# Opening, routing and first score rows of a recurrent attention and experts layer: statistics in pairs, score rows set between the routing's steps

## The chip, the cores and the metric

The kernel runs on one core of one Trainium2 chip. The metric is the device time of one execution in microseconds (us); the time before is the median of 3 runs. Engines: PE (TensorE, matmuls and turns, that is transposes by a matmul with the identity), DVE (VectorE), ACT (ScalarE), POOL (GpSimd), SP (SyncE, which here only issues transfers). ACT and POOL issue transfers too.

## The reference, cut to what matters

```python
x = L0_attn_x                                   # (8, 1024, 256), f32
xn = layernorm(x)
# attention over the 4 heads of each token (not over tokens)
q, k, v = ((xn @ W + b).reshape(b, s, h, d) for W, b in ((Wq, bq), (Wk, bk), (Wv, bv)))
qr, qi, kr, ki = q * cos(phase), q * sin(phase), k * cos(phase), k * sin(phase)
scores = (einsum('bshd,bsgd->bshg', qr, kr) + einsum('bshd,bsgd->bshg', qi, ki)) / sqrt(d)
out = einsum('bshg,bsgd->bshd', softmax(scores), v)
s = swapaxes(out, 1, 2).reshape(b, s, h * d) @ Wo + bo
# 8 experts, each token goes to its best 2
r = (einsum('btd,ed->bte', xn, router_w) + router_b) / max(temperature, 0.1)
for _ in range(3):                              # Sinkhorn
    r = r - logsumexp(r, axis=-1); r = r - logsumexp(r, axis=-2)
gates = normalised(exp(r)); vals, idx = top_k(gates, 2)
expert(e) = (relu(xn @ wg[e]) * (xn @ wp[e])) @ wo[e]
g = silu(xn + sum of the two chosen experts, weighted by normalised vals)
result = x + s * g
```

## The kernel before, in words

The 8192 tokens are 64 tiles of 128 rows; four tiles are a block, so there are 16 blocks. All arithmetic is f32, and the trace shows each f32 matmul as two records (a turn as one). The core's work comes in five stages.

**Set-up** (`fetch_setup`, `setup_scores`): small tensors and w_qk (the weights of queries and keys) are loaded. From the phases a 4 by 4 mix of heads for each column is made (`mixrow`), and from mix, biases and turned weights a linear map `lin` (256 rows by 8 + 16 columns): one product of a normalised row with `lin` gives the 8 routing scores and the parts of the 16 head scores that are linear in the row. In L263 to L285 those 16 columns are made by matmuls of four columns each, with a turned 128x128 piece of the weights as the stationary side.

**Opening** (`prepare`, `linear`; 16 blocks): for a block, bn_stats and bn_aggr (DVE L391, L392) give mean and variance of the rows, ACT takes the square root (L393), DVE the reciprocal and the shift (L396, L397); the rows are normalised in place by DVE (L408) and ACT (L403) in turns, PE turns them (L412), ACT copies the turned tile out of PSUM (L415), and POOL issues the stores of the turned rows (xT_d, from block 3 on) and of the normalised rows (xn_d). Each four blocks `linear` runs `lin` over them (L434), turns the result back (L445) and adds the offsets into `lg` (L448). x_0 to x_6 lie in the pool "prep", x_7 to x_11 in buffers of the attention, x_12 to x_15 in a pool "tail" that takes the space of the set-up. Behind the opening the list of entries in memory is filled with padding (L1097), and xn_d is copied to z_d (L1102).

**Routing** (`route`, `order`): 14 steps on one [128, 64, 8] tensor, nearly all on DVE, with three ACT functions (Exp L489, Ln L492, Exp L499, each with a table load) and four sums or maxima over all rows on POOL (L496, L507). `order` works out, for each token and choice, its place in the experts' list; `place` pieces (L643) and POOL's 128 indirect stores (`scatter`, L646) write the list, 8 stores to a piece. Beside it `setup_values` folds Wv and Wo into w_vo: turns of w_v (L295), matmuls pw (L329), ACT copies (L338), and the bias b_vo. Its tiles w_v, wT_v, w_o, bo_all lie in buffers of the attention (tags qk, u, junk).

**Attention** (`score`, `soften`, `value`; a generator `att_gen` whose yields are its steps). A tile's scores are nine steps: four of matmuls py (L666) with an ACT copy into qk (L673), one of four products (DVE L679), four of mixed keys kx (DVE L704) with their products (L679). There are two qk buffers, two kx buffers, and two PSUM buffers for py and pw together (tag "y"). A block behind, a tile's values are three steps: matmuls pu (L749), DVE adds (L756), matmuls po_s (L781), ACT copy. `run(att_gen, n)` sets n steps at that place of the program: 32 behind the first `place` piece, 15 behind each of the other 15, and 13: 270 steps ahead of the experts. The other steps are spread among the experts.

**Experts** (`experts`): 71 groups of 256 list entries; rows are gathered by POOL, three matmuls with their weights, and an indirect add into z_d. At the end `finish` joins x, attention and experts block by block.

**What sets the order.** The program is reordered when it is built: on each engine an instruction is put where it is expected to be ready, and among the ready ones the earlier in the program goes first. So the memset of L317, written in `setup_values`, runs at 7.49 us, and one pair of the matmuls of the first values (L749) at 97.03 us, between pw. `with tc.issue_after(ins)` keeps the instructions in its block behind `ins` on their engine. On the chip each engine then works in that order.

Of the kernel before, what the change touches and what calls it, by code (L numbers as in the profile page):

```python
# [9 lines left out]
F32 = mybir.dt.float32  # L10
AF = mybir.ActivationFunctionType
ALU = mybir.AluOpType
# [18 lines left out]
def recurrent_kernel(  # L31
# [127 lines left out]
    LATE = 3  # L159
    KEPT = 3  # L160
# [15 lines left out]
    def setup_scores(pool, rows, rw):  # L176
# [45 lines left out]
        mbk = pool.tile([P, KD, H, H], F32, name="mbk")  # L222
        mbq = pool.tile([P, KD, H, H], F32, name="mbq")
# [23 lines left out]
        for c in range(KD):  # L247
            nc.vector.tensor_scalar(mix[:, c], mix[:, c], 1.0 / math.sqrt(D), None, ALU.mult)
            nc.vector.tensor_tensor(mbk[:, c], mix[:, c], second(bkT, c), ALU.mult)
            nc.vector.tensor_tensor(mbq[:, c], mix[:, c], first(bqT, c), ALU.mult)  # L250
            nc.vector.tensor_tensor(mbb[:, c], mbk[:, c], first(bqT, c), ALU.mult)
# [9 lines left out]
        nc.vector.tensor_copy(off[:, E:], pl[:, :HH])  # L261
        lk = pool.tile([P, KD, H, H], F32, name="lk")
        for which, m in ((0, mbk), (1, mbq)):  # L263
            pl = ps_tr.tile([P, 512], F32, tag="tr", name=f"pl_lin_{which}")
            for k in range(KD):
                for a in range(H):
                    at = (k * H + a) * H
                    for c in range(KD):
                        nc.tensor.matmul(
                            pl[:, at : at + H],  # L270
                            wT[which][:, a, c, k * P : (k + 1) * P],
                            m[:, c, a] if which == 0 else m[:, c, :, a],
                            start=(c == 0),
                            stop=(c == KD - 1),
                        )
            flat = pl[:, : KD * HH]
            if which == 0:
                nc.vector.tensor_copy(lk.rearrange("p k h g -> p (k h g)"), flat)
            else:
                nc.vector.tensor_tensor(  # L280
                    lin[:, :, E:NL].rearrange("p k (h g) -> p k h g", h=H),
                    lk,
                    flat.rearrange("p (k g h) -> p k h g", k=KD, g=H),
                    ALU.add,
                )  # L285
        return bvT

    def turned(wT, part, name):

        for h in range(H):  # L290
            pt = ps_tr.tile([P, 512], F32, tag="tr", name=f"ptr_{name}_{h}")
            for c in range(KD):
                for k in range(KD):
                    at = c * D + k * P
                    nc.tensor.transpose(  # L295
                        pt[:, at : at + P], part(k, h)[:, c * P : (c + 1) * P], ident
                    )
            copy = nc.scalar.copy if h % 2 else nc.vector.tensor_copy
            copy(wT[:, h].rearrange("p c e -> p (c e)"), pt)

    def setup_values(bvT):

        w_v = att.tile([P, KD, HD], F32, tag="qk", name="w_v")
        with tc.issue_after(newest["rstd"].ins):
            nc.scalar.dma_start(w_v, wv.rearrange("(k p) n -> p k n", p=P))
        wvT = att.tile([P, H, KD, D], F32, tag="qk", name="wT_v")
        w_o = []
        for n in range(2):
            t = att.tile([P, R, D], F32, tag="u", name=f"w_o_{n}")
            half = wo[n * R * P : (n + 1) * R * P]  # L310
            with tc.issue_after(newest["rstd"].ins):
                nc.scalar.dma_start(t, half.rearrange("(k p) n -> p k n", p=P))
            w_o += [t[:, k] for k in range(R)]
        bo_all = att.tile([P, D], F32, tag="junk", name="bo_all")
        nc.gpsimd.dma_start(bo_all[:1], bo.unsqueeze(0))
        share = att.tile([P, D], F32, tag="junk", name="bo_share")
# [3 lines left out]
        turned(wvT, lambda k, h: w_v[:, k, h * D : (h + 1) * D], "wT_v")  # L320
        yield
        for i in range(R):
            for k in range(KD):
                for half in range(2):
                    pw = ps_y.tile([P, 512], F32, tag="y", name=f"pw_{i}_{k}_{half}")
                    for gg in range(2):
                        g = half * 2 + gg
                        for c in range(KD):
                            nc.tensor.matmul(  # L329
                                pw[:, gg * D : (gg + 1) * D],  # L330
                                wvT[:, g, c, k * P : (k + 1) * P],
                                w_o[i * KD + c],
                                start=(c == 0),
                                stop=(c == KD - 1),
                            )

                    with tc.issue_after(newest["shares"].ins) if i >= R // 2 else nullcontext():
                        nc.scalar.copy(w_vo[:, k, i, half * 512 : (half + 1) * 512], pw)  # L338
                yield
# [32 lines left out]

    def prepare(blk: int, pool):
# [10 lines left out]
        stats = small.tile([P, TB, 6], F32, tag="stats", name=f"stats_{blk}")  # L384
        mv = small.tile([P, TB, 2], F32, tag="mv", name=f"mv_{blk}")
        rstd = small.tile([P, TB], F32, tag="rstd", name=f"rstd_{blk}")
        shift = small.tile([P, TB], F32, tag="shift", name=f"shift_{blk}")
        for t in range(TB):

            with tc.issue_after(newest["trig"].ins) if not blk else nullcontext():  # L390
                nc.vector.bn_stats(stats[:, t, :], xt[:, t, :])  # L391
            nc.vector.bn_aggr(mv[:, t, :], stats[:, t, :])  # L392
        norm = nc.scalar.activation(rstd, mv[:, :, 1], AF.Sqrt, bias=eps)  # L393
        if blk < 8:
            newest["rstd"] = norm
        nc.vector.reciprocal(rstd, rstd)  # L396
        nc.vector.scalar_tensor_tensor(shift, mv[:, :, 0], -1.0, rstd, ALU.mult, ALU.mult)  # L397
# [30 lines left out]
    def linear(blk: int, pool):  # L428
# [15 lines left out]
        for t in range(TB):  # L444
            nc.tensor.transpose(  # L445
# [10 lines left out]
    def route(pool, hot, entries):  # L456
# [32 lines left out]
        nc.scalar.activation(ex, la, AF.Exp)  # L489
# [54 lines left out]
    def order(pool, hot, keep, placed):  # L544
# [4 lines left out]
        before = pool.tile(full, F32, name="o_before")  # L549
# [488 lines left out]
    turned_rows, x_tiles, all_scored = {}, {}, []  # L1038
# [36 lines left out]
    with tc.tile_pool(name="prep", bufs=2) as prep:  # L1075
        with tc.tile_pool(name="setup", bufs=1) as setup:
# [7 lines left out]
            bvT = setup_scores(setup, *small_rows)  # L1084
            prepare(0, prep)
        with tc.tile_pool(name="tail", bufs=1) as tail:
            for blk in range(12, T // TB):
                fetch_rows(blk, tail, f"x{blk}", 1)
            for blk in range(1, 4):
                prepare(blk, prep)  # L1090
            linear(0, prep)
            for blk in range(4, T // TB):
                prepare(blk, prep)
                if blk % 4 == 3:
                    linear(blk - 3, prep)
# [6 lines left out]
    copied = nc.sync.dma_start(z_d[: B * S], xn_d[: B * S])  # L1102
    tc.add_to_no_dep_group("padding", copied.ins)
    nc.sync.dma_start(
        z_d[B * S :].rearrange("(p m) d -> p m d", m=M),
        blank.unsqueeze(1).to_broadcast([P, M, D]),
    )
    with tc.tile_pool(name="routing", bufs=1) as routing:
        hot = routing.tile([P, E, K, T], F32, name="hot")
        entries = routing.tile([P, K * T * 2 + LE], F32, name="entries")  # L1110
        nc.vector.memset(entries, 0.0)
        for n in range(K):
            nc.vector.tensor_copy(pairs_of(entries)[:, n, :, 0], ids)

        keep = routing.tile([P, E, K * T], F32, name="keep")
        nc.vector.memset(keep, 1.0)
        nc.vector.memset(keep[:, :, :1], 0.0)

        values = setup_values(bvT)
        for n, _ in enumerate(route(routing, hot, entries)):  # L1120
            if n > 2:
                run(values, 1)

        with tc.issue_after(newest["columns"].ins):
            for m in range(M):
                pad = nc.gpsimd.indirect_dma_start(
                    xn_d,
                    bass.IndirectOffsetOnAxis(ap=padding[:, m : m + 1], axis=0),
                    blank,
                    None,  # L1130
                )
                tc.declare_no_dep(pad.ins, group="padding", reason="rows behind those copied")
                tc.add_to_no_dep_group("padding", pad.ins)
        placed = []
        run(order(routing, hot, keep, placed))
        run(values)
        put = scatter(entries, placed[0])
        next(put)
        run(att_gen, 32)
        for _ in put:  # L1140
            run(att_gen, 15)
        run(att_gen, 13)
# [67 lines left out]
```

## Time and profile before

| what | value |
|---|---|
| median of 3 runs | 1700.5 us (1699.61 to 1701.88) |
| the profiled execution | 1709.65 us, span 1707.8 us |
| PE busy | 1638.0 us, 96% |
| DVE busy | 1204.1 us, 71% |
| ACT, POOL busy | 429.7 us, 638.3 us |
| mean granted clock of PE | 0.978 |
| first turn of a block (PE L412) | 33.02 us |
| last addition into lg (DVE L448) | 87.37 us |
| first step of the routing (DVE L482) | 91.80 us |
| first place piece (DVE L643) | 148.09 us |
| first fetch of the experts' entries (POOL L859) | 396.33 us |
| 500 to 1500 us | PE busy 997.5 of 1000 us |

Times in the trace count from the first instruction; the device time of the same execution is 1.85 us more than its span. The granted clock is the share of full speed that the throttle gave PE. A "wait" is the idle time of an engine ahead of an instruction, with what ended it; it says nothing of cost where that engine isn't the one that sets the end.

### The profile page before, as it was taken

How to read it: one execution, taken by the hardware profiler on the slowest of the kernel's cores; microseconds unless marked ns; L12 is line 12 of the kernel's file. 1: busy time of each engine (PE TensorE's matmuls, PEld its weight loads, DVE VectorE, ACT ScalarE, POOL GpSimd, SP SyncE). 2: the span in 40 equal slices, each digit the busy share in tenths (PEclk: the TensorE clock that was granted, in tenths of full speed). 3: DMA queues.
4: the chain of work that ended last, by engine and by line, in shares of the span. 5: the costliest groups of instructions: out<-in, count | busy, mean ns of one | idle time of the engine just before them, and what ended most of it. 6: DMA issues, size and time to landing. Idle time of an engine off the chain costs nothing.

```text
span 1707.8 us, 22900 instructions
## 1 busy us (share of the span) xinstructions
PE 1638.0 (96%) x7697; PEld 1008.0 (59%) x7697; DVE 1204.1 (71%) x3704; ACT 429.7 (25%) x814; POOL 638.3 (37%) x599
## 2 busy tenths in 40 slices
PE   6897899999999999999999999999999999999986
PEld 5373344444666666766666666666666666767632
DVE  5769999997667566665757657576675756655776
ACT  3741212121222212222222222222222222222131
POOL 0312466566333434333434234343333433442212
PEclk8798999999999999999999999999999999999998
DMA  8993022114544544544544545455455445455489
GB/s 268 360 352 114 28 61 64 60 50 124 152 117 125 141 127 115 163 123 112 156 110 109 151 137 135 124 121 145 121 133 148 121 116 143 121 136 139 138 272 317
DMA packets 149161, 245.38 MB, mean 144 GB/s; under 512 B 15465, under 2 KB 93585, under 8 KB 148913
## 3 DMA queue, kind: packets, MB, share of 16 engines
q1 hardware_dynamic: 105648, 162.32, 29.6%
q0 software_dynamic: 41376, 77.38, 19.9%
q10 hardware_dynamic: 2016, 4.20, 0.7%
q8 instruction: 62, 1.02, 0.2%
q14 instruction: 59, 0.48, 0.1%
HBM read 176.85 MB, written 75.37 MB: 148 GB/s over the span
## 4 chain that ended last, share of the span: by engine, by line
PE 79%; DVE 14%; DMA 3%; issue 1%; ACT 1%; another core or an unknown queue 1%; POOL 0%; SPq 0%; ACTq 0%; POOLq 0%
PE py L666 23%; PE po L925 13%; PE pg L909 12%; PE pp L909 12%; PE pu L749 10%; DVE junk L679 5%; DVE kx L704 3%; PE po_s L781 2%; DVE w L768 2%; PE ptr_g L897 2%; DMA fz<-z_d 1%; PE po_s L776 1%; PE ptr_x L412 1%; DMA fo<-in_L_attn_x_dram 1%; DVE u L756 1%
## 5 line engine op out<-in xcount | busy, mean ns | idle before, releaser
L666 PE MATMUL py<-w_qk,xTa 128*128 128x512 f32 x1024 | 480.2, 605 | 15.9 <-ACT qk L673 14.3
L938 POOL DMA_INDIRECT z_d<-y,row x136 | 233.4, 1716 | 663.5 <-ACT y L935 642.8
L679 DVE CUSTOM_DVE_ANT_0 junk<-qk,kx,lg 128x256 f32<-128x256 f32 x768 | 323.9, 481 | 0.1
L666 PEld LDWEIGHTS py<-w_qk,xTa 128*128 128x128 f32 x1024 | 191.7, 193 | 213.8 <-issue 185.2
L679 DVE CUSTOM_DVE_ANT_0 junk<-qk,lg 128x256 f32<-128x256 f32 x256 | 113.6, 481 | 268.9 <-ACT qk L673 263.5
L673 ACT COPY qk<-py 128x512 f32<-128x512 f32 x256 | 149.2, 585 | 492.6 <-PE py L666 429.6
L909 PE MATMUL pg<-xgT,wg 128*128 128x256 f32 x1088 | 264.3, 385 | 0.2
L909 PE MATMUL pp<-xgT,wp 128*128 128x256 f32 x1088 | 260.6, 381 | 0.3 <-DVE hid L918 0.3
L749 PE MATMUL pu<-w_vo,xTa 128*32 128x512 f32 x2048 | 258.3, 598 | 1.1 <-DVE u L756 1.1
L925 PE MATMUL po<-wd,hid 128*128 128x256 f32 x1088 | 257.7, 382 | 0.0
L909 PEld LDWEIGHTS pg<-xgT,wg 128*128 128x128 f32 x1088 | 201.9, 190 | 84.1 <-issue 41.5
L925 PEld LDWEIGHTS po<-wd,hid 128*128 128x128 f32 x1088 | 203.2, 190 | 68.1 <-issue 44.4
L704 DVE TENSOR_TENSOR kx<-qk,mixrow 128x1024 f32<-128x1024 f32 (+1 forms) x256 | 233.8, 952 | 0.1
L909 PEld LDWEIGHTS pp<-xgT,wp 128*128 128x128 f32 x1088 | 204.4, 190 | 39.0 <-ACT hid L917 7.5
L646 POOL DMA_INDIRECT list_d<-entries,place x128 | 144.3, 1128 | 129.3 <-DVE place L643 94.7
L918 DVE TENSOR_TENSOR hid<-pp,hid 128x512 f32<-128x512 f32 x136 | 93.4, 687 | 138.1 <-PE pp L909 127.2
L768 DVE SCALAR_TENSOR_TENSOR w<-u,sc,w 128x256 f32<-128x256 f32 x444 | 185.9, 477 | 1.0
L872 POOL DMA_INDIRECT xg<-xn_d,row x136 | 151.6, 1115 | 57.1 <-issue 47.1
L917 ACT ACTIVATE hid<-pg 128x512 f32<-128x512 f32 x136 | 81.2, 597 | 297.2 <-PE pg L909 272.9
L749 PEld LDWEIGHTS pu<-w_vo,xTa 128*32 128x32 f32 x2048 | 58.8, 109 | 135.9 <-issue 128.2
L935 ACT ACTIVATE y<-po,entry 128x256 f32<-128x256 f32 x136 | 57.1, 470 | 256.2 <-PE po L925 251.6
L756 DVE TENSOR_TENSOR u<-pu,b_vo 128x512 f32<-128x512 f32 x128 | 86.2, 685 | 27.7 <-PE pu L749 27.4
(212 smaller groups left out, 999.7 us busy)
## 6 DMA issues: line engine op xcount, KB each, us to landing
wg<-in_L_ffn_wg_dram SPq DMA_DIRECT2D x68, 512.0 KB
wp<-in_L_ffn_wp_dram SPq DMA_DIRECT2D x68, 512.0 KB
wd<-in_L_ffn_wo_dram SPq DMA_DIRECT2D x68, 512.0 KB
list_d<-empty POOLq DMA_DIRECT2D x1, 9088.0 KB
x<-in_L_attn_x_dram SPq DMA_DIRECT2D x16, 512.0 KB
xn_d<-x POOLq DMA_DIRECT2D x16, 512.0 KB
s_d<-s_out SPq DMA_DIRECT2D x56, 128.0 KB
fo<-in_L_attn_x_dram SPq DMA_DIRECT2D x14, 512.0 KB
```

Of the source, the lines that this page charges most:

```text
L646: put = nc.gpsimd.indirect_dma_start(list_d, bass.IndirectOffsetOnAxis(ap=piece[:, c : c + 1], axis=0), entries[:, at * 2 : at * 2 + LE], ...
L666: newest["score"] = nc.tensor.matmul(py, xT[:, t, k], w[:, k, cols], start=(k == 0), stop=(k == KD - 1),)
L673: nc.scalar.copy(flat[:, cols], py)
L679: newest["dot"] = nc.vector.tensor_tensor_reduce(junk, qk[:, 0, h], k, 1.0 / math.sqrt(D), lg[:, tile_no, E + at : E + at + 1], ALU.mult, ...
L704: nc.vector.tensor_tensor(kx[:, :w], k, mixrow[:, at : at + w].unsqueeze(2).to_broadcast([P, w, 2, D]), ALU.mult,)
L749: nc.tensor.matmul(pu[i * J : (i + 1) * J, :], xT[:, t, k, i * J : (i + 1) * J], w_vo[:, k, i, cols], start=(k == 0), stop=(k == KD - 1),)
L756: nc.vector.tensor_tensor(u[:, cols], pu, b_vo.rearrange("p g d -> p (g d)")[:, cols], ALU.add)
L768: nc.vector.scalar_tensor_tensor(w[:, h], part, share, w[:, h], ALU.mult, ALU.add)
L872: nc.gpsimd.indirect_dma_start(xg[:, m], None, xn_d, bass.IndirectOffsetOnAxis(ap=row[:, m : m + 1], axis=0),)
L909: nc.tensor.matmul(dst[:, f], w[:, k, at : at + P], xgT[:, k], start=(k == 0), stop=(k == KD - 1),)
L925: nc.tensor.matmul(po[:, m], hid[:, f, m * P : (m + 1) * P], wd[:, f], start=(f == 0), stop=(f == KF - 1),)
L938: add = nc.gpsimd.indirect_dma_start(z_d, bass.IndirectOffsetOnAxis(ap=row[:, m : m + 1], axis=0), y[:, m], None, compute_op=ALU.add,)
```

## The change

**Set-up.** The matmuls of the linear map are turned round: the 4-column pieces, set in zeroed strips of 32 columns (`strips`), are the stationary side, and the turned weights move, 256 columns wide; the four heads go to four strips of 32 PSUM rows. ACT copies the result, PE turns it (four turns), DVE takes the columns out.

```diff
+        strips = att.tile([P, 2, KD, H, LW], F32, tag="mixer", name="strips")
+        nc.vector.memset(strips, 0.0)
...
+        for which in range(2):
+            for c in range(KD):
+                for a in range(H):
+                    nc.tensor.matmul(
+                        pl[a * LW : (a + 1) * LW, which],
+                        strips[which][:, c, a],
+                        wT[which][:, a, c],
+                        start=(c == 0),
+                        stop=(c == KD - 1),
+                    )
+        lT = rest.tile([P, 2, D], F32, tag="lT", name="lin_T", bufs=1)
+        nc.scalar.copy(lT, pl)
...
-        for which, m in ((0, mbk), (1, mbq)):
-            pl = ps_tr.tile([P, 512], F32, tag="tr", name=f"pl_lin_{which}")
-            for k in range(KD):
-                for a in range(H):
-                    at = (k * H + a) * H
-                    for c in range(KD):
-                        nc.tensor.matmul(
-                            pl[:, at : at + H],
-                            wT[which][:, a, c, k * P : (k + 1) * P],
...
```

**Opening.** The statistics leave `prepare` and become `measure`, which is called four blocks ahead; square root, reciprocal and shift are done for two blocks at once.

```diff
+    def measure(blk: int, pool):
+
+        pair, GT = blk // PAIR, PAIR * TB
...
+        if blk % PAIR == PAIR - 1:
+            norm = nc.scalar.activation(rstd, mv[:, :, 1], AF.Sqrt, bias=eps)
+            if blk < 2 * GROUP:
+                newest["rstd"] = norm
+            nc.vector.reciprocal(rstd, rstd)
+            nc.vector.scalar_tensor_tensor(shift, mv[:, :, 0], -1.0, rstd, ALU.mult, ALU.mult)
...
-            for blk in range(1, 4):
+            for blk in range(T // TB):
                 prepare(blk, prep)
-            linear(0, prep)
-            for blk in range(4, T // TB):
-                prepare(blk, prep)
-                if blk % 4 == 3:
-                    linear(blk - 3, prep)
+                if blk + GROUP < T // TB:
+                    measure(blk + GROUP, prep)
+                if blk % GROUP == GROUP - 1:
+                    linear(blk - GROUP + 1, prep)
+                if blk == GROUP:
+                    fetched_values = fetch_values(prep)
```

**Values.** w_v (in two loads) and w_o (two loads) are fetched into the slots of x in "prep" by `fetch_values`, wT_v into two more of them, bo_all into the slot of lT; `hot`, `keep` and `o_before` of the routing lie in slots of xT. The pool "prep" now lasts until the routing is done, and the routing's own pool takes the space of "tail". The matmuls pw are kept behind the last turn of `linear`, and the copies of w_vo behind an Exp of the routing.

```diff
+        w_v = [whole([P, HD], f"w_v_{k}") for k in range(KD)]
+        for k in range(KD):
+            with tc.issue_after(newest["rstd"].ins):
+                nc.scalar.dma_start(w_v[k], wv[k * P : (k + 1) * P])
...
+                            with tc.issue_after(newest["logits"].ins):
+                                nc.tensor.matmul(
...
-                    with tc.issue_after(newest["shares"].ins) if i >= R // 2 else nullcontext():
+                    done = (i * KD + k) * 2 + half
+                    behind = newest["shares" if done > 4 else "first"]
+                    with tc.issue_after(behind.ins) if done > 1 else nullcontext():
                         nc.scalar.copy(w_vo[:, k, i, half * 512 : (half + 1) * 512], pw)
```

Here "logits" is the last turn in `linear`, "first" the routing's first Exp, "shares" its second.

**Score rows.** Two steps of the attention are set behind each of the routing's 14 steps, and 28 fewer behind the first `place` piece; the 270 steps ahead of the experts stay 270.

```diff
             for n, _ in enumerate(route(routing, hot, entries)):
+
+                run(att_gen, 2)
                 if n > 2:
                     run(values, 1)
...
             put = scatter(entries, placed[0])
             next(put)
-            run(att_gen, 32)
+            run(att_gen, 32 - 2 * (n + 1))
             for _ in put:
                 run(att_gen, 15)
             run(att_gen, 13)
```

## The prediction, made before the changed kernel had run

> **What bounds the kernel now.** I read the chain of waits first, then busy time by stage, then the waits of the first 135 us engine by engine. The chain's shares by engine:
>
> ```profile
> PE 79%; DVE 14%; DMA 3%; issue 1%; ACT 1%; another core or an unknown queue 1%; POOL 0%; SPq 0%; ACTq 0%; POOLq 0%
> ```
>
> TensorE ends most of the span, and VectorE's 14% lies mostly ahead of the experts. Four stages show where (columns: stage, its length, busy us and instructions of each engine, granted clock, DMA share, GB/s):
>
> ```profile
> 33.00:88.00 55.00, 43.87 (x222) 23.41 (x223) 39.64 (x184) 38.73 (x82) 17.24 (x29) 0.75 0.91 342
> 88.00:132.00 44.00, 41.19 (x245) 28.38 (x243) 29.59 (x50) 17.61 (x28) 5.48 (x7) 1.00 1.00 353
> 132.00:205.00 73.00, 60.26 (x167) 24.89 (x168) 71.47 (x261) 14.43 (x27) 26.41 (x22) 0.88 0.17 58
> 205.00:396.00 191.00, 185.14 (x836) 79.43 (x834) 187.12 (x631) 40.27 (x78) 117.94 (x107) 1.00 0.20 59
> ```
>
> The opening (33 to 88) fills no compute engine: PE 43.9 of 55 us, DVE 39.6, ACT 38.7, while the DMA engines are at 0.91. In the routing (88 to 132) PE is full with the value weights, and DVE works 29.6 of 44. In 132 to 205 it is the other way round: DVE is full with score rows, PE idles 12.7 us and has only 0.88 of its clock. From 205 on both are full, and behind 396 PE alone (199 of each 200 us). So whatever lets DVE finish its part ahead of 205 earlier arrives at the end undiminished; but only as far as PE keeps up. The waits of DVE and of PE from 20 to 135 us (total, times, longest):
>
> ```profile
> DVE rstd L396 <- ACT rstd L393: 7.4, 8, 3.2
> ...
> DVE r_cm L506 <- ACT r_ex L499: 3.4, 1, 3.4
> DVE r_cs L511 <- POOL r_cs L507: 2.7, 3, 0.9
> DVE r_rs L491 <- ACT r_ex L489: 2.5, 1, 2.5
> DVE r_la L494 <- ACT r_rs L492: 2.4, 1, 2.4
> ...
> DVE entries L1111 <- DMA xn_d<-x: 1.5, 1, 1.5
> DVE r_la L498 <- POOL r_cg L496: 0.8, 1, 0.8
> ```
> ```profile
> PE ptr_x L412 <- ACT rstd L393: 6.6, 4, 1.7
> ```
>
> The routing's steps wait 11.8 us (3.4 + 2.7 + 2.5 + 2.4 + 0.8) for ACT and POOL with nothing else on DVE; in the opening PE waits 6.6 us for a block's standard deviation. The third item is in PE's timeline (start, us, instructions):
>
> ```profile
> 26.20 6.96 PE L269 MATMUL pl_lin<-mbq,wT 128*128 128x4 f32 x32
> 33.02 1.95 PE L412 MATMUL ptr_x<-ident,x 128*128 128x128 f32 x8
> ...
> 47.88 1.09 PE L412 MATMUL ptr_x<-ident,x 128*128 128x128 f32 x8
> ```
>
> The 64 narrow matmuls of L269 hold the first turn of a block back to 33.0 us, though its rows were normalised by 26.9.
>
> **Part 1: the linear map by strips.** Removed: 64 recorded matmuls, 22.4 to 33.2 us. Added: 32 records (each f32 matmul shows as two), 32 columns by 256, in four column strips. The nearest row is L749, same strips, twice as wide: 0.112 us a record, so 0.056, or 1.8 us (3.6 at half clock). Then a 0.59 us ACT copy, 8 records of turning (1.0 to 2.0 us) and two DVE steps of 0.2. The turns of block 0 need not wait for the last four, so they start at 22.4 + 1.8 to 3.6, say 25.5: 7.5 us earlier. The memset of the strips is some 0.5 us of DVE (384 columns took 0.38), in its wait for the first x.
>
> **Part 2: statistics four blocks ahead, in pairs.** The bn_stats and bn_aggr stay 128. Square root, reciprocal and shift fall from 16 of each to 8 of each: ACT saves 8 x 0.3 = 2.4 us, DVE 8 x (0.18 + 0.15) = 2.6 at most, as they overlap. PE's 6.6 us for rstd go. Engines alone would thus end the opening 14 us earlier. The transfers don't allow all of it: by the last store 16 x 0.52 (x) + 2.1 (w_qk) + 2.1 (w_v, w_o) + 16 x 0.52 (xn_d) + 13 x 0.52 (xT_d) = 27.8 MB must have moved; 9.0 of them had by 30 us (230, 355 and 312 GB/s). The remaining 18.8 MB take 45 us at the best slice of 10 us (414 GB/s) and 49 at 380: the last store lands at 75 to 79 instead of 90.3, when the entries memset was released. The routing's tiles now lie where the last x tiles were, so they still wait for it. I take 9 us, with 0 and 15 as ends.
>
> The row that weighs on this: 8 turns take 1.95 us at 33 us, where the clock is 0.50 for ten microseconds, and 1.09 at 47.9, right behind the wide matmuls of L434. The Trainium skill ("TensorE: Matmul & The Clock Gate", Part 4: PE-mode transpose) has turns not counted as work by the clock gate; by that, the opening's 128 turns stay at 0.244 us, 31 us, and with the 19 us of L434 and L445 PE needs 50 us, so the opening ends 5 us below before's and 7.5 by the earlier start: the good end of this part would be 12, not 15. It would also have wide matmuls between the turns lift the clock, which speaks against rival 2 below; the 9 us taken are worked out without it.
>
> **Part 3: value weights in the opening's x buffers.** w_v and w_o are now four loads on ACT's queue into slots of x_0 to x_3, so each waits until that block is stored, and an ACT instruction behind would wait too. Those stores are issued at 27.5 to 44.3 us, the loads behind the standard deviation of blocks 6 and 7 (some 45 us): cost 0, with up to 5 us (85.1 issue to 90.3 landing of the last store) if one lands late. The bias load moves on POOL's queue from 1.3 us to behind the last linear map: 0.65 us, in POOL's 12.7 us wait for r_cm. What it brings: the two qk buffers are free from the start. hot, keep and o_before go into xT slots whose blocks were stored 10 us before: 0.
>
> **Part 4: score rows between the routing's steps.** 28 steps of attention (4 of matmuls, 1 of diagonal products, 4 of others per row tile) are three tiles and one step; 4 of the 32 stay behind the first scatter piece. They issue no DMA: the first fetch of turned rows is in block 2. A tile costs DVE 10.0 us (first kx at 159.39 and 169.37), PE 16 x 0.43 = 6.9, ACT 4 x 0.585 = 2.3. So 30 us of DVE enter a chain with 11.8 us of holes. The sum on DVE is the same; the holes go, if a row is ready at each. Routing and order end later, the first place at some 91.8 - 9 + 26.7 + 30 + 12.5 = 152 us against 148.1; behind it waits POOL's scatter, 16 pieces of 11 us = 176, done by 330 and needed at about 378. So that delay is covered.
>
> Does PE keep up? From 88 to 205 PE has 15.5 us idle and 0.88 of its clock in 73 us (9 us); it can give 11.8 only while value weights and rows interleave. Both use the two py/pw buffers, and pw copies from the sixth on are issued behind the routing's second Exp, so once two buffers are full of pw, PE stands until then. The two first tiles' qk can be made in the opening, which covers most of it. I take 9 of the 11.8; ends 0 and 20 (rows taken into the opening's DVE idle time, 15 us).
>
> **Sum.** 1709.65 (profiled: span 1707.8 + 1.85) - 9 - 9 = 1691.7, 1.05% less. The median shown, 1700.5, lies 9 us below the profiled one; the same 18 us give **1682.5**.
>
> **Rivals.**
> 1. Only one part pays. Either the DMA engines, already at 0.91, hold the opening's end where it is, or PE has no room for rows in a stage in which it is 94% busy: 1700.5 - 9 = 1691.5. For it: share 1.00 of DMA behind 88. Against: share 0.50 from 30 to 40 us, a hole that fills when the last x loads are issued earlier.
> 2. Slower: nothing holds the rows' matmuls behind the opening, as "logits" holds the pw. From block 0's turn on they may be set between turns. At half clock 8 of them took 6.71 us at 166.95, so two tiles (two qk buffers) are 32 x 0.84 = 27 us of PE, against 11 idle there: the opening's end moves by 27 - 11 - 9 = +7 instead of -9. If DVE, still paced by later turns, gets nothing back: 1707.5. It decides when these matmuls are set there in numbers (over 20) and the clock stays at half. Against: a steady PE got its clock back (1.00 from 88 on), then they cost 14, and that is saved later.
> 3. The change doesn't do what it says: PE's queue puts all pw first, as now, and no row is ready in the routing; the opening alone gives 1691.5 as in 1.
>
> **How the numbers follow.** Forecast 0.55, its own range 1670 to 1689. Rivals 1 and 3 together 0.22, at 1691. Rival 2 and other losses 0.17. Both unknowns at their good ends (15 + 20 us, 1665) 0.03. Nothing to be seen 0.03. A measurement of this kernel tells 0.2%, 3.4 us, from no change. Part of the losses end within it: faster 0.79, same 0.05, slower 0.16. The range reaches from 1666 to 1704: below 0.03 to 0.05 are left out, above 0.12.
>
> **What would show it.** Right: the first turn at 25 to 26 us; last lg near 79; no ACT rstd among PE's waits; r_cm, r_rs and r_la with waits of under 4 us in all and score products between them; DVE over 95% from the routing's start to 205; first place near 150; first gather of the experts some 18 us earlier; stages behind it alike. Wrong: py matmuls between turns at 0.84 us; ACT standing at a w_v or w_o load; PE idle over 10 us between pw; DVE waiting for the store of a last x; the first place behind 175.

## The result and the profile after

| | before | after |
|---|---|---|
| median of the runs, same chip | 1700.05 us (4 runs, 1699.18 to 1701.88) | 1684.13 us (4 runs, 1682.64 to 1686.58) |
| ratio, 95% interval | 1 | 0.9905 [0.9893, 0.9917] |
| profiled execution, span | 1709.65 us, 1707.8 us | 1682.64 us, 1680.8 us |

The change takes 15.9 us, 1684.1 against 1682.5 forecast. The two profiled executions lie 27 us apart, 11 more than the medians, so their difference must not be read as the gain. Milestones of the two traces (start, us) show where the 27 arise:

| | before | after | difference |
|---|---|---|---|
| first turn of a block | 33.0 | 29.4 | -3.6 |
| last addition into lg | 87.4 | 74.6 | -12.8 |
| first step of the routing | 91.8 | 86.7 | -5.1 |
| second Exp of the routing | 105.4 | 107.8 | +2.4 |
| end of the routing's steps | 131.4 | 143.2 | +11.8 |
| first place piece | 148.1 | 157.8 | +9.7 |
| scores of block 0 done (ACT's Exp on them starts) | 187.5 | 169.3 | -18.2 |
| last place piece | 383.2 | 365.4 | -17.8 |
| first fetch of the experts' entries | 396.3 | 379.0 | -17.3 |
| first gathered rows turned (PE ptr_g) | 416.8 | 392.6 | -24.1 |
| end of the span | 1707.8 | 1680.8 | -27.0 |

The routing and the list end later than before, the score rows much earlier, and from "scores of block 0 done" to the experts the 18 us are carried unchanged. Between the last place piece and ptr_g the two traces move a further 6.4 us apart; that goes with a pause of ACT in the trace of before, and the last section tells why it isn't counted as gain. The chain of waits, by engine, against 79 and 14 before:

```profile
PE 81%; DVE 11%; DMA 2%; issue 1%; ACT 1%; POOL 0%; SPq 0%; POOLq 0%; DVEq 0%; ACTq 0%
```

The four stages as in the prediction (columns as there):

```profile
33.00:88.00 55.00, 49.09 (x257) 26.52 (x256) 42.85 (x178) 36.40 (x75) 17.79 (x29) 0.95 1.02 390
88.00:132.00 44.00, 37.12 (x133) 25.92 (x132) 33.87 (x74) 16.05 (x25) 5.27 (x7) 0.92 0.97 351
132.00:205.00 73.00, 62.99 (x297) 27.22 (x296) 71.33 (x247) 14.87 (x27) 36.48 (x33) 0.91 0.21 73
205.00:396.00 191.00, 190.97 (x871) 83.14 (x870) 185.17 (x624) 42.66 (x81) 121.48 (x116) 1.00 0.20 60
```

In the opening PE works 5.2 us more and its clock is 0.95 instead of 0.75; the DMA engines go from 0.91 to full (342 to 390 GB/s). In the routing DVE gains 4.3 us of work and PE gives 4.1 up. Behind 205 PE has 0.03 us idle of 191 (5.86 before) and DVE now has 5.8: PE has become the bound there. It is full from 182 on (23.00 of the 23.00 us from 182 to 205). What DVE still waits for from 20 to 135 us, and PE:

```profile
DVE junk L715 <- ACT qk L709: 4.3, 2, 3.0
DVE lg L484 <- PE ptr_l L481: 4.2, 3, 1.7
DVE r_cs L547 <- POOL r_cs L543: 2.7, 3, 0.9
DVE keep L1156 <- DMA xT_d<-xT: 2.5, 1, 2.5
DVE r_cm L542 <- ACT r_ex L535: 2.0, 1, 2.0
DVE r_rs L527 <- ACT r_ex L525: 2.0, 1, 2.0
DVE rstd L418 <- ACT rstd L415: 1.6, 1, 1.6
DVE r_la L530 <- ACT r_rs L528: 1.4, 1, 1.4
```
```profile
PE pw L352 <- ACT w_vo L363: 6.9, 1, 6.9
PE ptr_x L448 <- ACT xT L451: 2.5, 6, 0.6
```

No rstd is among PE's waits any more; one new wait of 6.9 us is. The routing's own steps still wait 8.1 us (2.7 + 2.0 + 2.0 + 1.4) of 11.8 before. And DVE's timeline ahead of the routing, which holds what the prediction did not think of:

```profile
76.45 0.48 DVE L715 CUSTOM_DVE_ANT_0 junk<-qk,lg 128x256 f32<-128x256 f32 x1
...
86.45 0.38 DVE L1151 MEMSET entries<- 128x384 f32 x1
86.74 0.36 DVE L518 TENSOR_SCALAR r_la<-lg,itemp 128x512 f32<-128x512 f32 x1
```

Between the last lg at 74.6 and the first step of the routing at 86.7 DVE hardly waits (0.7 us): from 76.45 to 86.4 it does score rows, while the last stores land (by 82.5, when SP's copy of z_d is released).

### The profile page after: what moved, and what is told of

It reads as the page before. It is cut to its first block, busy times and chain, and to the rows that moved or that the text cites. A ratio compares the mean times of both kernels' runs of the same rounds, so it can differ in the third digit from the quotient of the medians.

```text
span 1680.8 us, 22808 instructions
## 1 busy us (share of the span) xinstructions
PE 1621.0 (96%) x7669; PEld 997.0 (59%) x7669; DVE 1201.8 (72%) x3689; ACT 427.5 (25%) x807; POOL 635.3 (38%) x599
## 4 chain that ended last, share of the span: by engine, by line
PE 81%; DVE 11%; DMA 2%; issue 1%; ACT 1%; POOL 0%; SPq 0%; POOLq 0%; DVEq 0%; ACTq 0%
PE py L702 25%; PE po L961 13%; PE pg L945 12%; PE pp L945 12%; PE pu L785 12%; DVE junk L715 4%; PE po_s L817 3%; DVE kx L740 2%; PE ptr_g L933 2%; DVE w L804 2%; DMA fz<-z_d 1%; PE po_s L812 1%; DVE u L792 1%; DVE hid L954 1%; DVE w L808 0%
## 5 line engine op out<-in xcount | busy, mean ns | idle before, releaser
L792 DVE TENSOR_TENSOR u<-pu,b_vo 128x512 f32<-128x512 f32 x128 | 86.1, 683 | 27.5 <-PE pu L785 27.2
```

## The experiments

The main theory: two parts that pay about equally, the earlier opening and the rows; the rows pay by giving DVE score work in time that it waited, and what they push back (routing, list) is covered by POOL's scatter. Rivals: one part alone pays; or py matmuls among the turns cost time; or a wait made by the change eats part of the gain, and removing it gives a faster kernel. Kernels were run in three groups, each on one chip with the kernel before beside it (medians of before 1707.07 us for the first four, 1699.05 for the next four, 1709.75 for the last four), so ratios are compared, not times. One thing limits what the first and the last group show: in their traces ACT stands still for some 10 us at the start of the experts, and in 2, 4, 9, 10 and 12 also once or twice ahead of them (last section). The traces of the second group (5 to 8) and of the changed kernel have no such pause, so the split of the gain rests on these.

To compare traces ahead of those pauses, a mark on DVE is used: the first step of the softmax of block 0 (scm), which is ready when DVE has done block 0's score products. It is at 186.8 us before, 167.2 after and 167.1 in 5. From there to the last place piece it is 195 to 200 us in before, after, 1 to 3 and 5 to 8.

**1. Rows out of the routing.** All else as after; the 28 steps go back behind the first place piece.

```diff
-                run(att_gen, 2)
                 if n > 2:
                     run(values, 1)
...
-            run(att_gen, 32 - 2 * (n + 1))
+            run(att_gen, 32)
```

> The changed kernel with the 28 attention steps taken out of the routing and set behind the first place piece again (32 there); opening and buffers as changed. Theory (opening and rows pay separately: the last lg is 12.8 us earlier, the end of block 0's scores 18.2, so the rows give about 5): 1689 us, 5 slower than the changed kernel, with the routing's first step near 77 us and its waits of 11.8 us back. Rival A (the rows bring nothing, the opening all): 1684. Rival B (only rows turn the earlier opening into time, since DVE would otherwise wait for the last stores and for ACT and POOL): 1697 or more.

Measured: 1716.0 us, ratio 1.0058 [1.0044, 1.0072], slower than before, which neither theory had. PE's waits from 20 to 190 us, then DVE's:

```profile
PE pb_vo L370 <- DMA bo_all<-in_L_attn_bo_dram: 23.3, 1, 23.3
```
```profile
DVE o_sums L624 <- PE pq L621: 21.1, 1, 21.1
```

The bias load was issued on POOL's queue at 89.2 us, behind the padding of the list (9 MB) that was issued at 71.7, and its first user started at 131.55, 42 us after the issue. From 85 to 110 us the copy of z_d on SP's queue holds 97% of the DMA engines' time and POOL's queue 7%; from 112 to 126 POOL's queue alone moves 5.4 MB, and only then does the load land. On PE the matmuls of the list's order (pq) stand behind pb_vo, and on DVE the step o_sums behind pq. In the changed kernel the same load is issued at 96.1 and pb_vo starts at 133.7 without a wait: there the rows push PE's pw so far back that the bias, whose queue still moves data behind 126 us, is no longer late. The experiment therefore didn't separate the parts, and it raised a question for the changed kernel: does the late bias cost there as well? (5 and 6.)

**2. Old opening, rows kept.** The old narrow map, and the statistics again block by block, right ahead of the normalisation.

```diff
-    PAIR = 2
+    PAIR = 1
...
-            for blk in range(GROUP):
-                measure(blk, prep)
...
+                measure(blk, prep)
                 prepare(blk, prep)
-                if blk + GROUP < T // TB:
-                    measure(blk + GROUP, prep)
```

> The changed kernel with the opening of before: narrow matmuls for the linear map, statistics of one block right ahead of its turns; rows between the routing's steps and value weights in the opening's buffers as changed. Theory: the opening's part is lost, 11 us: 1695. Rival A (opening is everything): 1700. Rival B (the rows carry the gain, the opening only shifts waits): 1687.

Measured: 1702.45, ratio 0.9977 [0.9967, 0.9988]. First turn 33.6, last lg 88.0, as before; block 0's scores are done at 179.3 (187.5 before). PE's pb_vo waits 2.6 us for the bias.

**3. The kernel before once more**, as a kernel of this group, no edit.

> The kernel before, unchanged, for a second profile. Its first profile took 1709.65 us against a median of 1700.5, with PE idle 3.8 us and at half clock around 390 us. If that hole belongs to the order of the program, it is there again and the profile takes 1709; if it was chance (a late transfer), it is gone and the profile takes about 1700. Ratio to before: 1.000.

Measured: 0.9999 [0.999, 1.0009]; milestones within 2.3 us of the first trace up to the experts. Such a ratio is good to 0.1%.

**4. Value copies free.** The `issue_after` of the ACT copies of w_vo is taken out, which is behind PE's new wait of 6.9 us.

```diff
-                    behind = newest["shares" if done > 4 else "first"]
-                    with tc.issue_after(behind.ins) if done > 1 else nullcontext():
+                    if True:
                         nc.scalar.copy(
```

> The changed kernel without the rule that keeps the ACT copies of w_vo behind the routing's Exps, so that two full buffers of value weights no longer stop PE (6.9 us at 102 us in the changed kernel's profile). If PE is the limit of the routing: 5 us faster, 1679. Theory (DVE sets it, PE's idle time there costs nothing): within 2 us of 1684. If the copies now come ahead of the Exps on ACT and hold the routing: slower by the 1 to 3 us of one or several copies of 0.59 us.

Measured: 1728.4, ratio 1.0118 [1.0096, 1.0139]. DVE's waits from 85 to 180 us:

```profile
DVE junk L714 <- ACT qk L708: 20.1, 5, 9.7
```

PE runs 48 pw records in a row from 99.96 us on (10.5 us) while DVE stands ready for score rows; the routing ends at 169 instead of 143, and scm comes at 178.4, 11 us later than after. So the 6.9 us that PE waits go with PE's alternating between values and rows, and the theory that this wait eats part of the gain has fallen. The whole loss against the changed kernel is 36 us (2.1%). How much of the other 25 us the edit causes isn't shown: ACT stands for 21.2 us up to 231.9 (releaser "remote"), and PE for 15.1.

**5. Bias early.** The bias goes into a free row of b_vo, so its load needn't wait for the buffer and is issued in the set-up.

```diff
-        last = prep.tile([P, 2 * D], F32, tag="lT", name="bo_all", bufs=1)
-        bo_all, share = last[:, :D], last[:, D:]
+        bo_all, share = b_vo[:, 3], b_vo[:, 2]
```

> The changed kernel, but the bias bo lands in a row of b_vo that is still free, so its load is issued at the start (1.3 us, as before) instead of on POOL's queue behind the 9 MB of list padding. In the changed kernel's trace no matmul waits for it (pb_vo starts at 133.7 us), so theory: same as the changed kernel within 2 us, ratio to before 0.990. If the late bias held back more than the trace shows, or if the order that is built comes out better: up to 4 us faster, 0.988.

Measured: 1684.2, ratio 0.9913 [0.99, 0.9927]: no difference from the changed kernel that can be measured. The late bias costs nothing there. All following experiments but 7 have this edit, so that it doesn't decide them.

**6. The opening alone** (1 with 5).

> As e1_rows_back (no attention steps in the routing), with the bias loaded early. In e1 PE waited 23.3 us for the bias, and DVE 21.1 us behind it. Theory (that wait hid what the opening gives): 20 us less than e1, 11 less than before, ratio 0.993 to 0.994, with block 0's scores done near 173 us. Rival (the opening gives nothing without rows, since DVE has the same holes and only starts them earlier): ratio 0.998 or more.

Measured: 1689.53, ratio 0.995 [0.9936, 0.9963], 8.5 us (0.005 x 1700). It differs from 1 by the place of one 1 KB load (and the memset beside it), and by 1.1% in time. First turn 28.2, last lg 72.7, first place 133.7, block 0's scores done 174.2.

**7. Score matmuls held behind the opening.** The py of the first two tiles are kept behind the last turn of the logits; bias as in the changed kernel.

```diff
             for k in range(KD):
-                newest["score"] = nc.tensor.matmul(
+                with tc.issue_after(newest["logits"].ins) if tile_no < 2 else nullcontext():
+                    newest["score"] = nc.tensor.matmul(
```

> The changed kernel with the row matmuls of the first two tiles kept behind the last turn of the linear maps, so none stand among the turns. In the changed kernel 12 records of them stand there (30.8 to 44.5 us) and the clock is 0.94 in the opening against 0.75. If they cost what they take (12 x 0.43 to 0.86 us): the last lg comes 3 to 6 us earlier, and the routing has those matmuls to do: within 3 us of the changed kernel. If they keep the clock up (a turn took 0.13 to 0.24 us): the opening is no shorter and the rows are later, 3 to 6 us slower, ratio 0.993.

Measured: 1698.38, ratio 0.9992 [0.9983, 1.0001]: nearly the whole gain is gone. Without py among the turns the last lg comes 1.4 us earlier (73.2), but 1.1 of these are there at the first turn already (28.3 for 29.4), ahead of any py: from the first turn to the last lg it is 44.9 us here and 45.1 after. So the 15 py records that stand ahead of the last lg in the changed kernel cost 0.3 us, if anything. But DVE now has no row when it could use one; its waits from 20 to 181 us:

```profile
DVE junk L716 <- ACT qk L710: 17.8, 5, 6.7
DVE wT_v L311 <- PE ptr_wT_v L306: 4.7, 1, 4.7
```

Block 0's scores are done at 180.8 instead of 169.3. PE's timeline of this kernel in the opening, and of the changed kernel:

```profile
30.71 1.94 PE L448 MATMUL ptr_x<-ident,x 128*128 128x128 f32 x8 [1.23 <-ACT xTa L451]
32.92 1.94 PE L448 MATMUL ptr_x<-ident,x 128*128 128x128 f32 x8 [0.27 <-issue]
```
```profile
29.42 1.19 PE L448 MATMUL ptr_x<-ident,x 128*128 128x128 f32 x8 [1.48 <-issue]
30.82 3.29 PE L702 MATMUL py<-w_qk,xTa 128*128 128x512 f32 x4 [0.22 <-ACT xTa L451]
33.91 1.46 PE L448 MATMUL ptr_x<-ident,x 128*128 128x128 f32 x8
```

In blocks 1 to 3 eight turns take 1.94 us on their own here, and 1.46, 1.04 and 1.04 behind the py in the changed kernel. The granted clock from 25 to 75 us is 0.86 here and 0.93 there: the rows pay for themselves in the opening by lifting the clock.

**8. The rows alone** (2 with 5).

> As e2_old_opening (rows in the routing, the opening of before), with the bias loaded early; PE waited 2.6 us for it in e2. Theory: the rows alone give 4 + 2 us, ratio 0.996 to 0.997. If e2's other waits (7.1 for the copies of w_vo, 13.6 of DVE for qk) are what binds: 0.998 as e2.

Measured: 1694.0, ratio 0.9971 [0.9959, 0.9983], 5 us. With 6: 8.5 + 5 = 13.5 us apart, 14.8 (from 5) to 15.9 together. The rows on top of the new opening bring 0.9950 - 0.9913, 6 us. So the parts add up within the intervals (each some 2 us either way), and neither alone is the gain. The move of the value weights and buffers is in 5, 6 and 8 alike and was never taken back alone; if parts simply add, it comes out at 8.5 + 5 - 14.8 = -1.3 us, which can't be told from nothing.

**9. Old map only** (statistics four blocks ahead in pairs, rows and early bias as in 5).

> The changed kernel with an early bias load and the narrow four-column matmuls of the linear map as before; statistics in pairs, rows and buffers as changed. Theory: in the changed kernel the first turn stands 3.6 us earlier (29.4 for 33.0), so the last lg and the end come 3 to 4 us later than in e5_bias_early, ratio to before 0.9935. If the transfers (the last stores) set the routing's start anyway: within 1 us of e5, 0.9915. If all of the opening's 8.5 us hang on the map: 0.996.

Measured: 1710.26, ratio 0.9998 [0.9987, 1.0009]: the gain is gone, and by the ratio more of it than with the whole old opening (8). PE's timeline:

```profile
27.90 6.94 PE L272 MATMUL pl_lin<-mbq,wT 128*128 128x4 f32 x32
39.20 1.94 PE L439 MATMUL ptr_x<-ident,x 128*128 128x128 f32 x8 [4.36 <-issue]
```

The first turn is at 39.2, 5.7 us behind that of 8. DVE waits 6.2 us for these narrow matmuls with `lin`, and the statistics of a pair stand behind `lin` in DVE's order; ACT's first square root comes at 35.9, after a wait of 10.1 us for mv. So the pairs need the short map. By DVE's mark the old map costs the opening's whole part and little more: scm is at 177.1, 10 us behind 5 and 0.9 behind 8 (176.2). What 9 loses beyond 8 lies behind the mark: the Exp on block 0's scores starts at 185.2, since ACT stands until 182.6, and a second time until 244.5:

```profile
ACT qk L700 <- remote: 27.6, 5, 10.5
```

These are its waits of that kind from 150 to 250 us; 8 and the changed kernel have none there. From scm to the last place piece 9 takes 213 us, 8 198. Whether these pauses come from the order that was built or from the execution isn't shown, so the loss beyond 8 can't be put down to the edit. The traced execution of 9 is also the longest of its eleven (1716.4 us).

**10. Old statistics only** (one block at a time, right ahead of the normalisation; new map, rows, early bias).

> The changed kernel with an early bias load and each block's statistics right ahead of its turns, one block at a time, as before; linear map by strips, rows and buffers as changed. Theory: the square root's wait comes back, some 6 us: ratio 0.995. If rows' matmuls now fill that wait on PE: 2 us, 0.9925. If all of the opening's 8.5 us hang on the statistics: 0.996.

Measured: 1702.64, ratio 0.9957 [0.9944, 0.997], 7 us of gain left. The last lg is at 75.05, half a microsecond later than after: the opening is as short without pairs. PE has a new wait there:

```profile
PE ptr_wT_v L306 <- DVE wT_v L311: 4.6, 1, 4.6
```

But by DVE's mark little is lost: scm is at 168.8, 1.6 us behind 5, and the first place piece at 159.4, 1.6 behind too. The Exp on block 0's scores starts 7.5 us later than after (176.8), and the cause is again ACT, which stands for 10.5 us up to 174.3. Its waits of that kind from 150 to 180 us:

```profile
ACT qk L708 <- remote: 12.0, 2, 10.5
```

From scm to the last place piece 10 takes 211 us, 5 198. So the pairs bring some 1.6 us as far as the trace is undisturbed, by free time on DVE and ACT; the rest of the 7 to 8 us that the ratios of 5 and 10 lie apart can't be put down to them. With 9 this says that most of the opening's part hangs on the map by strips.

**11. Three steps a time** (behind each of the first nine routing steps; early bias), **12. Values later** (value steps from the seventh routing step on, not the third; early bias): two ways to have more rows ready early.

```diff
-                run(att_gen, 2)
+                run(att_gen, 3 if n < 9 else 0)
...
-            run(att_gen, 32 - 2 * (n + 1))
+            run(att_gen, 32 - 27)
```
```diff
-                if n > 2:
+                if n > 6:
                     run(values, 1)
```

> The changed kernel with an early bias load and three attention steps behind each of the first nine routing steps (27) instead of two behind each of fourteen (28), so the second and third tile's matmuls go ahead of more of the value weights on PE. In the changed kernel DVE still idles 10 us from 87 to 143 us because no row is ready in the Sinkhorn steps. If ready rows are what is short: 3 to 6 us faster than e5, ratio 0.988 to 0.9895. If PE's total is the limit (it is full from 182 us on): within 2 us of e5, 0.991.

> The changed kernel with an early bias load and the value weights' steps starting four routing steps later, the last ones behind the order; so PE makes row products first. Theory: as e11, DVE's waits for qk in the routing fall, 0 to 5 us faster than e5, ratio 0.988 to 0.991. If the first values (block 0's, needed when its scores are done) then wait for w_vo: slower by up to the 7 us of the last four pw groups, 0.995.

Measured: 1699.53, ratio 0.9945 [0.9934, 0.9957], and 1707.68, ratio 0.9987 [0.9976, 0.9997]. Both lose. PE's waits of 11 (20 to 170 us), then of 12 (20 to 176):

```profile
PE pw L351 <- ACT w_vo L362: 10.1, 1, 10.1
```
```profile
PE ptr_wT_v L306 <- DVE wT_v L311: 13.3, 1, 13.3
```

In 12 DVE in turn waits 18.0 us for rows (junk behind ACT's qk, longest 12.4), and scm comes at 174.7, 7.6 us behind 5: put later, the value weights leave PE standing while DVE waits, and the rows come later. The rest of the 13 us between 12 and 5 comes behind that mark, where ACT stands for 9.9 us up to 213.1. In 11 scm is at 168.1, only 1.0 behind 5; most of its 5 us arise behind that, where PE waits 5.6 us in four pieces for nothing that the profile shows, so for 11 the cause of the loss stays open. No version was faster than the changed kernel.

## Why the prediction was right

The forecast was 1682.5 from two parts of 9 us each, taken off the median. Measured were 8.5 us for the opening alone, 5 for the rows alone and 6 for the rows on top; together 15 to 16. That the sum is off by only 2 us owes something to luck: the rows' term was 3 to 4 us too large and priced at a place where little of it arose.

- **The strips**: sized at 1.8 to 3.6 us; the 32 records took 0.62 + 1.93. Right. The first turn was put at 25.5 and came at 29.4; the term was 7.5 and measured 3.6. Two things were left out. The turns of block 0 stand behind the turning of the map on PE (ptr_lin at 27.28, after ACT's copy): in 10, where block 0's first rows are normalised by 23.3, the first turn comes at 27.2. And the pairs make block 0 wait: its standard deviation is now taken together with block 1's, and DVE normalises its first row only here (at 22.2 before):

```profile
28.91 0.41 DVE L444 TENSOR_SCALAR x<-x,mv,rstd 128x256 f32<-128x256 f32 x1
```

The first turn follows 0.1 us behind, and so it does in all eight traces with strips and pairs. The 1.48 us that the view calls "issue" are this wait; the pairs take back some 2 us of what the strips give.
- **The opening's end**: last lg forecast near 79, measured 74.6. The prediction let the transfers set the end. The copy of z_d behind the last stores is issued at 82.6 us (91.2 before), 8.6 us earlier, the 9 that were taken; its own estimate of the landing, 75 to 79, was too early. Without rows the stores do set the routing's start (in 6 the entries memset waits 6.4 us for them, until 80.5); in the changed kernel they no longer do, since DVE is at its row tile until 86.4. The DMA engines had room for it, as the slice at 0.50 had suggested. That lg is ready 8 us ahead of the stores made room on DVE that no term had.
- **The rows**: the mechanism was wrong in its place, and the sum came out only 3 to 4 us too high. The holes should shrink from 11.8 us to under 4; they are 8.1. The waits of 2.7 us for POOL's sums, in three pieces of at most 0.9, were not touched. Instead DVE does a whole row tile between lg and the stores (76.5 to 86.4 us). The prediction had this only as the good end of a range ("rows taken into the opening's DVE idle time, 15 us"). DVE was to be over 95% busy from the routing's start to 205; from 88 to 205 it is 90% (33.87 + 71.33 of 117 us), against 86% before.
- **PE keeps up** only as long as it alternates: the prediction saw the two buffers and the guard and counted on the first tiles' qk from the opening. Experiments 4 and 7 show both halves: without the guard DVE's mark comes 11 us later, without qk from the opening 11.6 us, and there the kernel takes 14 us more.
- **The list's delay is covered**: first place at 157.8, not 150 to 152 (the routing starts at 86.7 instead of 82.8, and the order's part takes 14.7 us instead of 12.5), and still the last place piece is 17.8 us earlier. Right, and experiment 6 agrees: its first place is 24 us ahead of after's, and its last one 5 us behind.
- **The bias load** was priced at 0.65 us of POOL, in a wait. In this kernel that holds (5). But the price was looked for on the wrong side: the engine that issues, not the queue that carries. Experiments 1 and 6, with and without it, differ by 1.1%.
- **w_v and w_o, hot, keep, o_before** at nothing: the w_v loads are issued at 40.4 and 43.8 us, and no wait for them or for w_o is in the trace; the memset of keep waits 2.5 us for the store of xT, but at 65.5 to 68.0 us, where DVE has room. Right.
- **Rival 1 and 3** (only one part): fallen by 6 and 8. **Rival 2** (py among the turns makes it slower): py do stand among the turns from 30.82 us on, but 15 records up to the last lg, not the over 20 of its condition, and the clock doesn't stay at half. The first four took 0.82 us a record (clock 0.50 from 32 to 34 us); then the clock rises (1.00 from 36 to 40), and the whole costs 0.3 us of the opening at most (7). The Trainium skill ("TensorE: Matmul & The Clock Gate", Part 4: PE-mode transpose) has turns not count as activity for the clock gate; the rows of 7 (1.94 us for eight turns in blocks 1 to 3) and of after (1.46, then 1.04 behind py) agree with it. The prediction's estimate by that rule took 19 us for L434 and L445, which are 16.5 in the trace of before (13.91 + 2.57), and left all turns at 0.244 us; in the changed kernel many run at half of that. The 9 us taken didn't rest on it.
- **Where the rest went.** DVE has some 10 us of waits left between 87 and 143 us. The two ways tried to fill them with more rows (11 and 12) didn't: PE waited 10.1 and 13.3 us for the value weights instead. That PE is full from 182 us on speaks for PE as the next bound; no run lightens PE there to show it.

Left open: what makes ACT stand in 2, 4, 9, 10 and 12, and so how much of what 4, 9, 10 and 12 lose belongs to their edits; and what 11 loses behind DVE's mark.

## What to carry to other kernels

Work set into waits pays where an engine that is late later on is idle now; look for the longest stretch between two of its stages (here from the last lg to the landing of the stores, 8 us), not only for the small waits inside a chain. Two parts that feed each other are best tried in all four combinations: here taking the rows back (1) cost more than their share, by a wait for the bias that this made elsewhere and that 6 doesn't have. Where an edit loses more than its marks on the engines explain, look for a pause of the trace before putting it down to the edit (9, 10). When a small load is moved, ask what is ahead of it on the queue at its new place: 1 KB behind the list's padding was the difference between 0.5% faster and 0.6% slower.

## What the runs showed that was not expected

A load of 1 KB issued behind the padding of the list on the same queue was usable only 42 us later (89.2 to 131.5 us, experiment 1); issued early it makes nothing wait (5, 6).

The kernel before has a median of 1699 to 1700 us beside two sets of kernels (after; 5 to 8) and of 1707 to 1710 beside the other two. One visible part of it is a pause of ACT at the start of the experts, whose end the profile puts to "remote", that is to nothing in the trace that it can name. ACT's longest wait from 360 to 422 us in the trace of before:

```profile
ACT qk L673 <- remote: 9.8, 1, 9.8
```

All nine traces that belong to the longer times have it (the first one of before with 1709.65 us, 1 to 4 and 9 to 12; 9.4 to 9.8 us each); the five others (after, 5 to 8) don't. Where it is, the way from the last place piece to the first ptr_g takes 32.4 to 34.1 us, without it 27.2, whichever opening the kernel has. So 6.4 of the 27 us (33.6 - 27.2 in the first two) go with the pause and not with the change, and 1709.65 - 18 would have been the wrong base for the forecast; the median was the right one.

Pauses of the same kind stand ahead of the experts in five traces, all of them from the longer times: in 2 (6.5 us up to 335.2), 4 (21.2), 9 (10.5 and 10.4), 10 (10.5) and 12 (9.9). The way from DVE's mark to the last place piece takes 227 us in 4, 213 in 9, 211 in 10 and 206 in 12, against 195 to 200 in the nine traces named above (and 203 in 11, which has none of them). What the pauses are, and whether an order can bring them on, the runs don't show.
